# Four-layer image network on Trainium2: expectation values' products in one block, gathers two taps ahead, results consumed some steps later

## The chip, the cores and the metric

The kernel runs on one NeuronCore of one Trainium2 chip. The core has TensorE (PE: matrix products into PSUM), VectorE (DVE), ScalarE (ACT: activation functions), GpSimd (POOL: here it issues the gathers by index) and SyncE (SP: it issues all other transfers). Each works through its own list of instructions and waits at semaphores for the others. The metric is the time of one execution on the device, in microseconds (us); lower is better. Every number is float32.

## The reference, cut to what matters

The input is x of 16 images, 192 channels, 32 x 32 pixels. Four layers follow each other, each of the form x = x + layer(groupnorm(x)):

- layer 0: a recurrent block over the 1024 pixels, a linear layer, a 3 x 3 convolution, a batch norm over all images
- layer 1: attention. Each of 6 heads maps 32 channels of a pixel to 6 angles and these to a state of 64 amplitudes (a product of cosines and sines). Two fixed circuits w, one for queries and one for keys, turn the state; the squares of the amplitudes are probabilities, and their signed sums, projected to 4 numbers, are the query and key vectors. Softmax over the 1024 pixels follows
- layer 2: deformable convolution. A 3 x 3 convolution gives 18 offsets per pixel, and each of 9 taps reads the image at a shifted, fractional place (four corners with weights)
- layer 3: a gated feed-forward block with a 2 x 2 transform, a 3 x 3 convolution per channel and a GELU

The part of layer 1 that the first edit touches, in the reference:

```python
def _measure_z(state):
    probs = jnp.abs(state) ** 2
    return probs @ _ZSIGN.T
...
zq = _measure_z(_pqc(_pqc(state0, enc_w), q_w))
q_vec = _layernorm(zq @ q_proj_w.T + q_proj_b, ln_gamma, ln_beta)
```

The kernel folds the signs and the projection into one matrix `amat` of 64 amplitudes (real and imaginary part, so 128 rows) by 4 numbers.

## The kernel before, in words

**Two phases.** `phase_a` does layer 0 for all images and ends at about 3330 us. `phase_b`, which the change is in, does layers 1 to 3.

**Four streams.** `phase_b` ends with `weave`. It takes four generators, which issue instructions and yield a number at each pause: `vectors` (query and key vectors of layer 1), `attention` (its softmax), `layer2` (offsets, then gathers) and `layer3`. `weave` always continues the stream that has progressed least, where a yield counts as its number divided by the stream's weight. The weights are the sums of the yields of one image, so that all streams advance by one image at the same rate, and the third entries (1.27, 2.49, 3.78) hold each stream that many images behind the first. What `weave` gives is an order of priority. A scheduler in the layer below then puts each engine's instructions into a list, by that priority and by when it takes their operands to be ready, and it hands out buffers.

**Vectors.** For each image, three head pairs `pr` run one after the other. `products` builds the state `psi` of two heads on VectorE; TensorE transposes it (`ppsi`), ScalarE copies it (`psiT`). For the two circuits w and two halves of the pixels hf, TensorE applies the circuit (`pcirc`, L1059), and ScalarE squares it (`prob`, L1061, 128 x 1024: 512 pixels for each of two heads). The function `expect` (L1049) then makes `pz`: for each (w, hf) two matmuls of 128 rows by 32 columns by 512 pixels, one per head, added up in the 32 partitions of PSUM that start at q. The columns of `amat` that are used are shifted by head, so that head numbers land in different places and the sum keeps them apart. `expect` of one (w, hf) is issued one step after its Square; the four strips of 32 partitions are written at four different times. `pz` is allocated before the first circuit of the pair.

**Buffers.** In SBUF the tag `v4` has five buffers of 128 x 1024. It serves xb, y, vec1, vec2, psi and prob of `vectors` and xn and x1 of `attention`. In PSUM the tag `mm` has two banks of 128 x 512 for all small products (ppsi, pz, pxt, poffc, poff, pgn, pgv, pout, pdt and others), and `big` two tiles of 128 x 1024 for pmax, pscore, pcirc, paug and phad.

**Layer 2.** `layer2_offsets` normalizes, transposes and writes four shifted copies of the image as a table of rows to DRAM (`xg`), convolves for the offsets (`poffc`, L1303, four strips of 32 partitions for each of 9 taps), copies (`ot`, L1307), transposes (`poff`, L1310) and computes indices and weights on VectorE (`pos`, L1315, to `w4`, L1336). `layer2_gathers` goes through 4 blocks of pixels x 9 taps. For each tap GpSimd gathers two tiles `gt` (L1357, 6 buffers), ScalarE scales the first corner into `acc` (L1361, 5 buffers), VectorE adds three corners (L1387) and multiplies by the tap's weight (L1389), TensorE adds it up in PSUM (`pdef`, L1393).

**Group norm.** `groupstats` (L31 to L48) takes means on VectorE, averages over groups on TensorE (`pgn`), copies the result (`gm`, L37), and does the same for variances (`pgv`). All streams but attention use it.

**Layer 3.** `rows_in` makes four products `phad` (L1438); ScalarE scales two of them into `low` (L1445), VectorE combines with the others into `pad` (L1450); then come the convolution steps `dc` (L1487, L1489).

## Time and profile before

| | us |
|---|---|
| median of three runs | 9209.33 |
| lowest, highest | 9204.89, 9238.67 |
| the profiled execution, its own time | 9200.76 |
| its span, first to last instruction | 9199.0 |
| TensorE busy | 8010.2 (87%) |
| VectorE busy | 6945.0 (75%) |
| ScalarE busy | 4235.8 (46%) |
| GpSimd busy | 1784.4 (19%) |

The mean clock that TensorE was granted is 0.912 of full speed. By phase: from 0 to 3330 us TensorE is busy 3019.3 us and VectorE 2408.4; from 3330 to 8364 us (the last pz) 4464.3 and 3844.2 of 5034; from there to the end 526.5 and 692.4 of 835.

How to read the lines that follow: a group of instructions is given as line, engine, operation, output<-inputs with sizes, count, then busy time, mean duration in ns of one, and the idle time of the engine just before them with what ended most of it. A float32 matmul is recorded as two passes, so counts of matmuls in the profile are twice those of the program. Matmuls overlap: busy time is that of their union, and a mean duration is not a rate; the rate is read from one start to the next. In the stages' table the columns are the stretch, its length, and for each engine busy time and (count), then the granted clock, the DMA engines' mean busy share, and GB/s. A wait is given as engine, waiting tile and line <- releasing engine, tile and line: total us, times, longest us.

### The profile page before, as it was taken

Reading aid. Unit: us, or ns where it says so; the run is one execution under the profiler, and the core shown is the slowest. Engines: PE = TensorE matmul, PEld = TensorE weight load, DVE = VectorE, ACT = ScalarE, POOL = GpSimd, SP = SyncE. Lnnn points to the kernel's source line nnn. Section 1 sums busy time; section 2 is a strip of 40 time slices with the busy share of each in tenths; the row PEclk is TensorE's granted clock in tenths of the full one; section 3 lists DMA queues with packets and bytes.
Section 4 is the critical chain, followed back from the end, with each engine's and each line's share of the span. In section 5 each row is a group of like instructions: output and inputs, shape, how many; then the busy total and the mean of one; then the engine's idle time right before and its main releaser. Section 6 shows DMA issues by size and latency. Waiting matters only on the chain. (4 is left out here: it accounts for less than half of the span.)

```text
span 9199.0 us, 91391 instructions
## 1 busy us (share of the span) xinstructions
PE 8010.2 (87%) x30512; PEld 3387.7 (37%) x30512; DVE 6945.0 (75%) x14313; ACT 4235.8 (46%) x7395; POOL 1784.4 (19%) x1680
## 2 busy tenths in 40 slices
PE   5999999999999969998998988988988898988853
PEld 2555555555555532232333323323333233323221
DVE  6777777777777744668788778788788788778888
ACT  3444444444444424444454454444545444444432
POOL 0101000101001100222222222222222223223342
PEclk9899999999999979998998998999998998999965
DMA  1111111111111120433443443433333334334352
GB/s 50 43 43 45 44 43 50 43 43 46 44 43 50 40 55 21 136 122 103 125 129 95 134 124 100 128 115 117 119 118 119 118 113 124 120 103 131 118 159 64
DMA packets 301028, 814.44 MB, mean 89 GB/s; under 512 B 47579, under 2 KB 164381, under 8 KB 300555
## 3 DMA queue, kind: packets, MB, share of 16 engines
q0 software_dynamic: 92160, 453.06, 15.8%
q1 hardware_dynamic: 208395, 355.55, 12.4%
q8 instruction: 239, 3.92, 0.2%
q14 instruction: 234, 1.92, 0.1%
HBM read 667.13 MB, written 132.94 MB: 87 GB/s over the span
## 5 line engine op out<-in xcount | busy, mean ns | idle before, releaser
L1357 POOL DMA_INDIRECT gt<-xg,ix x1152 | 1463.8, 1271 | 4235.7 <-DMA xn<-xnd 1165.5
L1387 DVE SCALAR_TENSOR_TENSOR acc<-gt,w,acc 128x192 f32<-128x192 f32 x3456 | 1213.0, 410 | 173.4 <-ACT acc L1361 147.5
L1151 DVE TENSOR_REDUCE mx<-pmax 128x2 f32<-128x1024 f32 x768 | 934.8, 1218 | 431.8 <-PE pmax L1149 429.5
L1149 PE MATMUL pmax<-kt,qt 64*128 64x512 f32 x3072 | 1097.0, 671 | 174.2 <-ACT pexp L1191 83.6
L1188 PE MATMUL pscore<-qt,kt 64*128 64x512 f32 x3072 | 1017.7, 690 | 196.7 <-DVE mx L1151 109.7
L1191 ACT ACTIVATE pexp<-pscore 128x1024 f32<-128x1024 f32 x768 | 780.5, 1017 | 739.2 <-PE pscore L1188 732.3
L1361 ACT ACTIVATE acc<-gt,w 128x192 f32<-128x192 f32 x1152 | 497.9, 451 | 1281.2 <-DMA gt<-xg,ix 1007.5
L1180 PE MATMUL pav<-pexp,vo 128*64 128x512 f32 x3072 | 962.4, 658 | 80.9 <-ACT pexp L1191 57.2
L508 POOL COPY qbd<-qT 32x384 f32<-32x384 f32 x512 | 303.9, 594 | 2847.6 <-PE se L542 2762.7
L1489 DVE SCALAR_TENSOR_TENSOR dc<-pad,wdw,dc 128x512 f32<-128x512 f32 x1152 | 807.1, 742 | 9.5 <-ACT dc L1487 9.1
L1393 PE MATMUL pdef<-acc,ident 128*128 128x384 f32 x1152 | 597.3, 604 | 125.4 <-DVE acc L1389 111.1
L538 ACT ACTIVATE dm<-dm,wtm 128x128 f32<-128x128 f32 x1536 | 490.6, 388 | 348.0 <-DVE dm L494 268.6
L1149 PEld LDWEIGHTS pmax<-kt,qt 64*128 64x128 f32 x3072 | 315.6, 197 | 757.8 <-issue 202.1
L1188 PEld LDWEIGHTS pscore<-qt,kt 64*128 64x128 f32 x3072 | 286.5, 201 | 712.2 <-issue 300.8
L550 PEld LDWEIGHTS pintra<-v,pt 128*128 128x128 f32 x3072 | 428.6, 213 | 164.1 <-issue 71.0
L550 PE MATMUL pintra<-v,pt 128*128 128x33 f32 x3072 | 437.7, 291 | 2.4 <-DVE pt L545 2.4
L1180 PEld LDWEIGHTS pav<-pexp,vo 128*64 128x64 f32 x3072 | 172.0, 141 | 662.9 <-issue 504.1
L1393 PEld LDWEIGHTS pdef<-acc,ident 128*128 128x128 f32 x1152 | 194.2, 210 | 563.2 <-DVE acc L1389 225.1
L545 DVE SCALAR_TENSOR_TENSOR pt<-se,dm 128x512 f32<-128x512 f32 x384 | 263.0, 685 | 144.5 <-PE se L542 143.5
L1049 PE MATMUL pz<-prob,amat 128*32 128x512 f32 x768 | 366.5, 603 | 0.9 <-ACT prob L1061 0.9
L1061 ACT ACTIVATE prob<-pcirc 128x1024 f32<-128x1024 f32 x192 | 195.6, 1020 | 351.3 <-PE pcirc L1059 344.8
L542 PE MATMUL se<-qbd,kT 64*128 64x256 f32 x1536 | 292.4, 450 | 54.1 <-DVE pt L545 54.1
(423 smaller groups left out, 12848.3 us busy)
## 6 DMA issues: line engine op xcount, KB each, us to landing
dm<-gd SPq DMA_DIRECT2D x128, 768.0 KB
xg<-xt SPq DMA_DIRECT2D x224, 192.0 KB
gt<-xg,ix POOLq DMA_INDIRECT x1152
xb<-x_in SPq DMA_DIRECT2D x32, 384.0 KB
y<-ydram SPq DMA_DIRECT2D x32, 384.0 KB
x1d<-xb SPq DMA_DIRECT2D x32, 384.0 KB
xnd<-y SPq DMA_DIRECT2D x32, 384.0 KB
xn<-xnd SPq DMA_DIRECT2D x48, 256.0 KB
```

Of the source, the lines that this page charges most:

```text
L538: nc.scalar.activation(dm[:, h, :], dm[:, h, :], AF.Exp, bias=wtm[:, c, 64 + h:65 + h])
L550: nc.tensor.matmul(pa[:, hh * 33:hh * 33 + 33], pt[:, h * 128:(h + 1) * 128], v33[:, hh, :], start=True, stop=True)
L1149: nc.tensor.matmul(pm[:, hh, :], qT[r, tt * 128:(tt + 1) * 128], kT[r, hf * HS:(hf + 1) * HS], start=True, stop=True)
L1151: nc.vector.tensor_reduce(mx[:, tt, hf, :], pm, AX.X, ALU.max, negate=True)
L1180: nc.tensor.matmul(po[0][hh * 64:hh * 64 + 64], vo[:, tt, hh * 32:hh * 32 + 64], pe[:, hh * HS:(hh + 1) * HS], start=(tt == 0), stop=(tt = ...
L1188: nc.tensor.matmul(ps[:, hh * HS:(hh + 1) * HS], kT[r, tt * 128:(tt + 1) * 128], qT[r, s], start=True, stop=True)
L1191: nc.scalar.activation(pe, ps, AF.Exp)
L1357: nc.gpsimd.indirect_dma_start(out=gt, out_offset=None, in_=xg, in_offset=bass.IndirectOffsetOnAxis(ap=ix[:, c:c + 1], axis=0))
L1361: nc.scalar.activation(acc[:, j, :], gt[:, 0:192], AF.Copy, scale=w4[:, 0, c:c + 1])
L1387: nc.vector.scalar_tensor_tensor(acc[:, j, :], gt[:, cr * 192:(cr + 1) * 192], w4[:, cr, c:c + 1], acc[:, j, :], ALU.mult, ALU.add)
L1393: nc.tensor.matmul(po[:, 0:384], cn.ident, acc.rearrange("p j c -> p (j c)"), start=(t == 0), stop=(t == 8))
L1489: nc.vector.scalar_tensor_tensor(out, src, w, add, ALU.mult, ALU.add)
```

## The change

It has four parts.

1. In `vectors`, the four `prob` of a head pair are kept, and all eight matmuls into `pz` are issued together after the last Square: first the four strips for one head, then the four for the other. `pz` is allocated just before. `products` of the next pair is issued after this block instead of before the last `expect`. The pauses change from 2.5 to 2.0 after each circuit, and to 3.0 and 1.0 behind the block.
2. In `layer2_gathers`, `first` is split into `read` (the gathers) and `first` (ScalarE's scaling). The gathers of tap n + 2 are issued in the step of tap n, the scaling of tap n + 1 as before in the step of tap n. A pause of 4.0 stands between the first two reads and the first scaling.
3. Pauses are added before a result of another engine is used: 1.0 before the group means are copied; 3.0 before, 2.0 after and 4.0 later around the offsets' copy and transposes; 2.0 instead of 1.0 between `low` and `pad`.
4. The weights of three streams are set to the new sums of their pauses.

```diff
@@ groupstats
     nc.tensor.matmul(pg[:96, 0:2], cn.g6, mv[:, :, 0], start=True, stop=True)
+    yield 1.0
     gm = pool.tile([96, 2], F32, tag="gngm", name="gngm")
@@ phase_b
-        weave([(stream(0, vectors), 86.0), (attention(g), 205.8, 1.27), (layer2(g), 155.5, 2.49),
-               (stream(3, layer3), 131.9, 3.78)])
+        weave([(stream(0, vectors), 87.0), (attention(g), 205.8, 1.27), (layer2(g), 169.5, 2.49),
+               (stream(3, layer3), 136.9, 3.78)])
@@ vectors
-        pz = mm("pz")
-        def expect(w, hf, prob):
-            q = (w * 2 + hf) * 32
-            for hh in range(2):
-                o = 20 - (pr * 2 + hh) * 4
-                nc.tensor.matmul(pz[q:q + 32, :], g.amat[:, w, o:o + 32], prob[:, hh * HS:(hh + 1) * HS],
-                                 start=(hh == 0), stop=(hh == 1))
-        ready = None
+        prob = {}
         for w in range(2):
             for hf in range(2):
...
-                prob = v4("prob")
-                nc.scalar.activation(prob, pc, AF.Square)
-                yield 2.5
-                if ready:
-                    expect(*ready)
-                ready = w, hf, prob
+                prob[w, hf] = v4("prob")
+                nc.scalar.activation(prob[w, hf], pc, AF.Square)
+                yield 2.0
+        pz = mm("pz")
+        for hh in range(2):
+            o = 20 - (pr * 2 + hh) * 4
+            for w in range(2):
+                for hf in range(2):
+                    q = (w * 2 + hf) * 32
+                    nc.tensor.matmul(pz[q:q + 32, :], g.amat[:, w, o:o + 32], prob[w, hf][:, hh * HS:(hh + 1) * HS],
+                                     start=(hh == 0), stop=(hh == 1))
+        yield 3.0
         if pr < 2:
             psi = products(pr + 1)
-        yield 2.0
-        expect(*ready)
         if pr == 0:
...
+        yield 1.0
@@ layer2_offsets
         yield 2.0
+    yield 3.0
     ot = g.xp("ot")
     nc.scalar.activation(ot, po, AF.Identity)
+    yield 2.0
     pf = mm("poff")
...
+    yield 4.0
     n = 144
@@ layer2_gathers
-    def first(n):
+    def read(n):
         block, t = taps[n]
         part = []
-        acc = g.pairs("acc")
         for j in range(2):
...
+        return part
+    def first(part):
+        acc = g.pairs("acc")
         for j, gt, c in part:
             nc.scalar.activation(acc[:, j, :], gt[:, 0:192], AF.Copy, scale=w4[:, 0, c:c + 1])
-        return acc, part
+        return acc
...
-    coming = first(0)
+    reads = [read(0), read(1)]
+    yield 4.0
+    firsts = [first(reads[0])]
     for n, (block, t) in enumerate(taps):
-        (acc, part), coming = coming, first(n + 1) if n + 1 < len(taps) else None
+        if n + 2 < len(taps):
+            reads.append(read(n + 2))
+        if n + 1 < len(taps):
+            firsts.append(first(reads[n + 1]))
+        acc, part = firsts[n], reads[n]
@@ layer3, rows_in
                 nc.scalar.activation(low[j], ph[:, 1, j, :], AF.Copy, scale=g.fft[:, 2 + j, ab, gt:gt + 1])
-            yield 1.0
+            yield 2.0
```

## The prediction

> **What bounds the kernel now.** I read the page first (busy shares, slices, costliest groups), then the busy time by stretch of one steady image, the timeline of TensorE, and the waits by engine. The chain that ended last reaches back only to 9024 us, so it tells about the drain and not about the stretch that the change touches; I leave it aside. Lines of the page, busy tenths in 40 slices of 230 us, then the group that is re-ordered:

> ```profile
> PE   5999999999999969998998988988988898988853
> DVE  6777777777777744668788778788788788778888
> PEclk9899999999999979998998998999998998999965
> ...
> L1049 PE MATMUL pz<-prob,amat 128*32 128x512 f32 x768 | 366.5, 603 | 0.9 <-ACT prob L1061 0.9
> ```

> From slice 16 on (phase B, 3330 us to the end) neither engine is at 9 throughout: TensorE holds 8 to 9, VectorE 7 to 8. Over 3330 to 9199 they are busy 4991 and 4537 of 5869 us. So the question is which of the two is full where pz stands. The mapping of pz to images repeats: an image takes about 350 us (first gathers at 6522, 6870, 7225 us). The stretches of one image, from the view by stages:

> ```profile
> core 0: us, PE busy (x) PEld busy (x) DVE busy (x) ACT busy (x) POOL busy (x), PEclk, DMA share, GB/s
> 6570.00:6606.00 36.00, 34.99 (x123) 13.45 (x124) 24.46 (x48) 18.15 (x34) 6.04 (x7) 1.00 0.40 124
> 6606.00:6642.00 36.00, 30.49 (x105) 8.81 (x103) 34.65 (x70) 15.73 (x28) 9.76 (x6) 0.95 0.26 79
> 6690.00:6810.00 120.00, 99.42 (x321) 34.14 (x319) 114.27 (x228) 62.38 (x96) 30.13 (x24) 0.91 0.32 98
> 6785.00:6870.00 85.00, 81.57 (x325) 23.62 (x325) 58.49 (x102) 41.29 (x50) 3.66 (x4) 0.95 0.25 74
> 6870.00:6894.00 24.00, 21.79 (x68) 7.67 (x68) 20.48 (x52) 12.55 (x22) 16.61 (x13) 1.00 0.80 259
> ...
> ```

> The stretch without gathers (6785 to 6870, offsets being computed) is full on TensorE: 81.6 of 85 us, VectorE 58.5. In 6570 to 6606 TensorE is full too (35.0 of 36, VectorE 24.5). VectorE is the full one in 6690 to 6810 (114.3 of 120). The same view of pz alone gives 11.42 us x24 in 6785 to 6870, 6.06 us x13 in 6570 to 6606 with 1.55 just after, and 3.06 us x7 in 6870 to 6894: the 48 recorded pz matmuls of an image (12 products, two matmuls each, recorded as two passes) lie nearly all where TensorE is full.

> The timeline of TensorE shows what they cost next to a block of the same shape that is already on four strips, the offset convolution:

> ```profile
> 3730.80 1.90 PE L1049 MATMUL pz<-prob,amat 128*32 128x512 f32 x4
> 3732.64 1.13 PE L1149 MATMUL pmax<-kt,qt 64*128 64x512 f32 x4
> ...
> 3735.29 1.07 PE L1303 MATMUL poffc<-xpad,woff 96*32 96x512 f32 x8
> 3736.29 1.13 PE L1149 MATMUL pmax<-kt,qt 64*128 64x512 f32 x4
> ```

> From start to next start: 4 pz in 1.84 us, 0.46 each; 8 poffc in 1.00 us, 0.125 each. Both last 592 ns apiece; poffc overlaps about four at a time.

> [...] poffc here shows 3.7x for four. [...] 192 pz visits become 48, which no row prices, so I count nothing.

> **The change, part by part.** *Products in one block.* Before, a head pair has four visits of 1.84 us = 7.36. After, one visit of 8 matmuls, first the four strips of the first head, then of the second: the built order has 48 blocks of 8, none split. 16 passes at 0.125 = 2.0, with the tail of the last 2.1. Saved: 5.3 us a block, 3 x 16 blocks = 254 us of TensorE. That is the ceiling for this part. What is on the path:
> - 6785 to 6870, half the products: 11.0 us becomes 3.1, saved 7.9. TensorE is full, and the gathers wait for the offsets at its end. Two of the six products stand before 6810, where VectorE is full as well: I take off half of their 2.6, and count 6.6.
> - 6570 to 6606, four products: saved 5.3; VectorE has 11.5 us to spare: whole.
> - 6870 to 6894, two products: saved 2.6; VectorE is at 20.5 of 24: half, 1.3.

> Sum 13.2 us an image. In the VectorE-full stretches that follow nothing shrinks, and half-rate clock may take some back: I keep nine tenths, 11.9, times 16 images = 190 us. With all 5.3 of each block it would be 254, with the chain to the offsets alone (see the rivals) 96. The first images' products (from 3381 us) lie where TensorE is at 462 of 500 us, so they count alike. After the last pz (8364 us) the remaining 835 us stay.

> *Waits that the block adds.* It needs all four Squares. In the built order other matmuls stand between the last circuit product and the block; at the trace's rates 4.0, 8.7 and 6.8 us for the three head pairs. A Square lasts 1.02 us, so it is covered unless ScalarE is late. The next psi is issued behind the block; 11.4 and 16.4 us of matmuls stand before its transposes. Without that cover the price is what ScalarE is late by; behind pz on TensorE are the scores, and ScalarE's exponentials wait for those.

> *Buffers.* Four prob and vec2 fill all five v4 buffers, so the attention's xn load, x1 loads and psi are taken before or after a block. SyncE's order stays nearly the same; the second x1 load now has some 5 us of VectorE work ahead of its use instead of 13, and I count 0 to 1 us. In PSUM, pz holds one of the two mm banks for a block instead of a whole pair; waits such as pout for xo (16.6 us in 4500 us) shrink: at most 1 us an image.

> *Gathers two taps ahead, pauses and weights.* The waits in 4000 to 8500 us (13 images), from the waits by engine:

> ```profile
> ACT acc L1361 <- DMA gt<-xg,ix: 795.1, 431, 6.4
> ...
> DVE pos L1315 <- PE poff L1310: 197.7, 13, 15.3
> DVE pad L1450 <- ACT low L1445: 120.2, 40, 5.9
> ...
> DVE gngm L37 <- PE pgn L35: 61.0, 15, 6.1
> ...
> PE pscore L1188 <- DVE pad L1450: 24.1, 8, 5.9
> ```

> ScalarE waits 61 us an image for gathers, VectorE 15 for the offsets, 9 for low, 5 for the norm. By the text all of these should shrink. The built order says little moves: GpSimd still holds 72 gathers an image in the same order and six buffers; between a gather and its first reader stand 46 instructions of all engines on average instead of 43; VectorE reaches pos behind the same work plus one addition, pad behind low at 9 instead of 10, gngm at 7 instead of 6.5. ScalarE's wait is the one that TensorE feels (pexp behind acc). A tenth of 61 us less, a third of it felt: 2 us an image, 32 us in all at the high end, 0 or a few us lost at the low end (the pauses only move work). I take 10 us. The weights of the four streams only match the longer sums of their pauses.

> Sum: 9200.8 (the profiled execution; span 9199.0 and 1.8 around it) - 190 - 10 = 9001. The median of the runs (9209.3) stands 8.5 us above the profiled time, so about 9010; I say 9005, since both halves taken off above err to the slow side.

> **Rivals.** *More than the block:* moving work out of ScalarE's waits frees VectorE's stretches too, because one late gather stops all three (the waits for low and pad above are such cases). TensorE's six largest waits for ScalarE are 217 us in these 13 images, 16.7 each. If half of that goes as well: 8.3 x 16 = 133 less, about 8870. Against it: the built order hardly moves the gathers. *Given back in VectorE:* only the chain to the offsets gains. Five products stand before poff in its stretch, 9.2 us; after, one block and one more circuit product, 3.2: 6.0 us an image, 96 in all: 9113. For it: VectorE is busy 224 of the 263 us with gathers, and 114 of 120 after the first block. Against: the products are not there. *Slower:* the block becomes a wait. Its fourth Square stands in ScalarE's queue behind an acc, and TensorE stands still. It decides when the wait exceeds the 5.3 us saved; at the longest wait of acc for pdef, 6.9 us in every block, it costs 48 x 1.6 = 77: 9286. Against: the first pair's block, with the least cover, is in the stretch without gathers. *It doesn't do what it says:* the strips don't overlap with 128 rows as with 96: 9209. Against: pav, with 128 rows on two strips, already has 4 in 1.01 us, though each lasts about 0.6.

> **How the numbers follow.** Block as worked out 0.62 (own range 8940 to 9070), more 0.13, given back 0.13, slower 0.06, no overlap 0.06. About 0.5% (46 us) is what a measurement here can tell. The range takes in the likeliest case, the given-back case and half of the better one: 8880 to 9130. Faster by over 0.5%: the first three, less a little of the third, 0.87; within 0.5%: no overlap and that little, 0.07; slower 0.06.

> **What would show it.** Right: pz busy falls from 366 us to about 105, as 48 blocks of 16 in about 2 us; the stretch without gathers shrinks from 85 to about 77 us and an image from 350 to about 338; waits for pos and for gathers stay within a quarter. Wrong: blocks of 7 us (no overlap); TensorE idle before pz with prob as the releaser (slower); unchanged length with TensorE idle in its place and VectorE full (given back); waits of ScalarE for gathers halved (more).

## The result: half a per cent slower, with TensorE relieved as planned

| | before | after |
|---|---|---|
| median of seven runs, us | 9209.33 | 9261.55 |
| lowest, highest | 9195.97, 9238.67 | 9243.35, 9278.42 |
| profiled execution, its time and span | 9200.76, 9199.0 | 9250.15, 9248.3 |
| TensorE busy | 8010.2 | 7865.4 |
| mean granted clock | 0.912 | 0.904 |

The ratio is 1.0049, 95% interval 1.003 to 1.0068. I had forecast 9005, so the forecast was wrong by 257 us and in its sign.

The page of the changed kernel, busy tenths by slice as before:

```profile
PE   5999999999999969888888888888888888888853
DVE  7777777777777744767877778778678778778778
PEclk9899999999999979999898898998898998999865
```

From slice 17 on TensorE has fallen from "8 or 9" to 8 in nearly every slice. It has less to do, and the run is longer all the same. The group of the moved matmuls, from the groups by line of TensorE, and then TensorE's timeline at one block:

```profile
L1061 PE MATMUL pz<-prob,amat 128*32 128x512 f32 x768 | 96.0, 599 | 0.0
```

```profile
6829.88 1.92 PE L1061 MATMUL pz<-prob,amat 128*32 128x512 f32 x16
6831.73 1.13 PE L1146 MATMUL pmax<-kt,qt 64*128 64x512 f32 x4
```

So the block does what it says: 16 passes in 1.85 us to the next start, pz busy 96.0 in place of 366.5, and no idle time ahead of it (the last number of the group, 0.0). The stages of one image, gathers, then no gathers (the latter from the start of VectorE's last corner sum of an image to that of its first of the next); ahead of them the stretch with gathers of the kernel before:

```profile
core 0: us, PE busy (x) PEld busy (x) DVE busy (x) ACT busy (x) POOL busy (x), PEclk, DMA share, GB/s
6522.00:6785.00 263.00, 230.14 (x774) 82.57 (x772) 224.33 (x466) 130.89 (x218) 84.45 (x69) 0.92 0.44 134
...
6538.00:6807.00 269.00, 226.51 (x740) 82.14 (x739) 223.31 (x464) 132.75 (x219) 95.68 (x69) 0.88 0.42 130
6807.00:6896.00 89.00, 81.87 (x359) 24.39 (x356) 58.06 (x102) 42.77 (x52) 3.97 (x4) 0.95 0.24 71
```

The stretch without gathers took 85 us before and takes 89 here. The one with gathers has its TensorE 42 us short of full and a clock of 0.88, against 33 us and 0.92 before. One image is not the mean: over the ten images from the third to the twelfth the stretch without gathers grew from 85.1 to 91.5 us, and the one with gathers from 266.3 to 267.8. Waits in 4000 to 8500 us, first of ScalarE and VectorE, then of TensorE, and then two rows of TensorE's in the kernel before:

```profile
ACT acc L1363 <- DMA gt<-xg,ix: 834.3, 367, 8.7
...
DVE xo L1526 <- PE pout L1533: 230.9, 12, 19.2
...
DVE pad L1459 <- ACT low L1454: 104.2, 34, 5.1
...
DVE gngm L38 <- PE pgn L35: 89.6, 12, 8.9
PE pav L1177 <- ACT pexp L1188: 85.5, 32, 5.4
...
PE pcirc L1050 <- DVE mx L1148: 63.7, 27, 4.8
```

```profile
PE pav L1180 <- ACT pexp L1191: 26.7, 14, 3.9
...
PE pcirc L1059 <- DVE mx L1151: 0.9, 4, 0.2
```

VectorE's wait for pos (197.7 us in 13 times before) is down to 15.0 us in a single one, but in its place VectorE stands 19 us an image at xo, the instruction that is now ahead of pos, for pout. On TensorE, pav waited 26.7 us for the exponentials before and waits 85.5 now, and pcirc for the maxima 63.7 in place of 0.9. Not every wait grew: that of pscore for the maxima fell from 98.2 to 59.7.

To say where the time of an image went, I take from each trace the ten images from the third to the twelfth and split their mean length in three: *work*, TensorE's busy time with the part at half clock counted half; *half clock*, the other half of that part (the granted clock in these two traces is 1.0 or 0.5 at any time, in 316 spells before and 410 after); and *idle*, the rest. The three add up to the image by construction.

| us per image | image | work | half clock | idle |
|---|---|---|---|---|
| before | 351.4 | 288.2 | 25.3 | 37.9 |
| after | 359.2 | 276.2 | 31.5 | 51.5 |

Work fell by 12.0 us an image. Idle time grew by 13.6 and the loss to half clock by 6.2. Work is the time that TensorE was busy, which depends on how matmuls overlap, and is no constant of the program: over all the runs without the block it lies between 286.6 and 296.2 us, with the block and no other change of matmuls between 273.5 and 280.7.

### The profile page after: what moved, and what is told of

It reads as the page before. It is cut to its first block, busy times and chain, and to the rows that moved or that the text cites. A ratio compares the mean times of both kernels' runs of the same rounds, so it can differ in the third digit from the quotient of the medians.

```text
span 9248.3 us, 91393 instructions
## 1 busy us (share of the span) xinstructions
PE 7865.4 (85%) x30512; PEld 3365.6 (36%) x30512; DVE 6926.5 (75%) x14313; ACT 4283.4 (46%) x7433; POOL 1982.9 (21%) x1680
## 5 line engine op out<-in xcount | busy, mean ns | idle before, releaser
L1355 POOL DMA_INDIRECT gt<-xg,ix x1152 | 1660.9, 1442 | 4098.2 <-DVE w L1336 1790.3
L1146 PE MATMUL pmax<-kt,qt 64*128 64x512 f32 x3072 | 1075.4, 682 | 229.0 <-ACT pexp L1188 125.4
L1185 PE MATMUL pscore<-qt,kt 64*128 64x512 f32 x3072 | 1056.2, 687 | 161.1 <-DVE mx L1148 73.9
L1188 ACT ACTIVATE pexp<-pscore 128x1024 f32<-128x1024 f32 x768 | 780.3, 1018 | 803.8 <-PE pscore L1185 801.0
L1177 PE MATMUL pav<-pexp,vo 128*64 128x512 f32 x3072 | 1003.9, 671 | 121.4 <-ACT pexp L1188 116.3
L1498 DVE SCALAR_TENSOR_TENSOR dc<-pad,wdw,dc 128x512 f32<-128x512 f32 x1152 | 804.3, 742 | 15.3 <-ACT dc L1496 14.8
L1146 PEld LDWEIGHTS pmax<-kt,qt 64*128 64x128 f32 x3072 | 296.9, 198 | 831.0 <-issue 245.3
L1398 DVE TENSOR_TENSOR acc<-acc,wdef 128x384 f32<-128x384 f32 x576 | 317.1, 550 | 3.8
```

Source lines behind the costliest of these rows:

```text
L1146: nc.tensor.matmul(pm[:, hh, :], qT[r, tt * 128:(tt + 1) * 128], kT[r, hf * HS:(hf + 1) * HS], start=True, stop=True)
L1177: nc.tensor.matmul(po[0][hh * 64:hh * 64 + 64], vo[:, tt, hh * 32:hh * 32 + 64], pe[:, hh * HS:(hh + 1) * HS], start=(tt == 0), stop=(tt = ...
L1185: nc.tensor.matmul(ps[:, hh * HS:(hh + 1) * HS], kT[r, tt * 128:(tt + 1) * 128], qT[r, s], start=True, stop=True)
L1188: nc.scalar.activation(pe, ps, AF.Exp)
L1355: nc.gpsimd.indirect_dma_start(out=gt, out_offset=None, in_=xg, in_offset=bass.IndirectOffsetOnAxis(ap=ix[:, c:c + 1], axis=0))
L1498: nc.vector.scalar_tensor_tensor(out, src, w, add, ALU.mult, ALU.add)
```

## First round: which part lost it

Three theories. A: the pauses at the offsets push the transposes poff down TensorE's list, and the gathers wait for what follows from them. B: the block's gain is given back where VectorE is full. C: gathers two taps ahead collide with other transfers. For A stands TensorE's timeline after the last offset convolution:

```profile
6874.12 1.07 PE L1300 MATMUL poffc<-xpad,woff 96*32 96x512 f32 x8
...
6883.19 3.67 PE L1533 MATMUL pout<-gelu,wout 128*96 128x512 f32 x8
6886.70 0.60 PE L1309 MATMUL poff<-ident,ot 128*128 128x128 f32 x4
```

From the last poffc to poff it is 12.6 us. In the kernel before it is 3:

```profile
6858.04 1.07 PE L1303 MATMUL poffc<-xpad,woff 96*32 96x512 f32 x8
6859.03 1.08 PE L1180 MATMUL pav<-pexp,vo 128*64 128x512 f32 x4
6860.04 1.13 PE L1188 MATMUL pscore<-qt,kt 64*128 64x512 f32 x4
6861.10 0.66 PE L1310 MATMUL poff<-ident,ot 128*128 128x128 f32 x4
```

**The changed kernel without the offset pauses** (weight of layer2 160.5; in all runs the weights follow the sums of the pauses):

```diff
-    yield 3.0
     ot = g.xp("ot")
     nc.scalar.activation(ot, po, AF.Identity)
-    yield 2.0
     pf = mm("poff")
...
-    yield 4.0
     n = 144
```

> The changed kernel without the three pauses around the offsets' copy and transposes (3.0, 2.0, 4.0; layer2's weight 169.5 less 9 = 160.5), all else kept. Theory A, the pauses push the transposes poff some 10 us of matmul work behind the convolution (11.6 instead of 2.0 in the built order), and the gathers start that much later: the stretch without gathers falls from 90 to about 79 us, the time by 16 x 8 = 130 us to about 9130. Rival B, the loss is in the stretch with gathers, which VectorE fills: the time stays within 20 us of 9260. Rival C, the gathers ahead of time cost it: also about 9260.

Measured: 9048.38, ratio to before 0.9823 (0.9806 to 0.984). It is 213 us faster than the changed kernel and beats both kernels. That is more than A had forecast, though in the mean of the ten images the stretch without gathers fell by 8 us (91.5 to 83.5) and not by 11; the one with gathers fell by 9 (267.8 to 259.0). Its stages:

```profile
6778.00:7033.00 255.00, 221.44 (x764) 79.46 (x756) 225.25 (x469) 131.22 (x218) 85.14 (x69) 0.93 0.47 141
7033.00:7117.00 84.00, 79.84 (x337) 24.08 (x341) 56.52 (x99) 41.23 (x50) 3.30 (x4) 0.91 0.23 68
```

**The block alone** on the kernel before (edit: the block of the diff, nothing else; weight of vectors 86.0).

> The kernel before with the block of eight products alone (with its own pauses; the weight of vectors stays 86.0). Theory A with the gain as I predicted it: 9209 - 190 = about 9020. Rival B, the products' gain in the stretch with gathers is given back to VectorE and only the chain to the offsets gains, 5 to 6 us an image: about 9120. If the block is what makes the changed kernel slow: over 9240.

Measured: 9207.36, ratio 0.999 (0.9981 to 0.9999). Both A and B had expected a gain here, and the third line a loss. Neither came: the block alone earns nothing that counts.

**The offset pauses alone** on the kernel before (weight 164.5).

> The kernel before with the three offset pauses alone (layer2's weight 164.5). Theory A: poff stands 13.8 us of matmul work behind the convolution instead of 2.0, so 16 x 9 to 12 us more: 9350 to 9400. Rivals B and C: within 30 us of 9209.

Measured: 9406.11, ratio 1.0213 (1.0195 to 1.0231). The pauses cost 190 us without any other edit.

**One tap ahead** in the changed kernel:

```diff
-    reads = [read(0), read(1)]
-    yield 4.0
-    firsts = [first(reads[0])]
+    coming = first(0)
```

> The changed kernel with gathers issued one tap ahead as before, without the pause of 4.0 (layer2's weight 165.5). Theory A: within 30 us of 9260, since the offset pauses stay. Rival C, the gathers two taps ahead collide with other transfers (their mean issue time rose from 1271 to 1442 ns): about 9150.

Measured: 9127.1, ratio 0.9915 (0.9893 to 0.9937), 134 us faster than the changed kernel. It looked like C; it is not, as the last round shows. Nor does the time follow the gathers' own length, which C had pointed to: in the traces one takes 1442 ns in the mean in the changed kernel, but 1385 in a version below that takes 9092 us and 1343 in the one that takes 9406.

## Second round: the block's company

The block alone gives 0 and the version without offset pauses gives 168, so something beside the block matters. Four combinations without offset pauses:

> The kernel before with the block of products, the pause of 1.0 in the group norm and the pause of 2.0 in place of 1.0 after the low transform; one tap ahead, no pauses at the offsets (the planner's costs follow: 87.0, 156.5, 136.9). Without the offset pauses the change took 9048, and the block alone 9207, so some 159 us come from early gathers, from these two pauses, or from the block together with one of them. Gathers earn it: 9205, as the block alone. The two pauses earn it: about 9050. The block earns it, but only where something else fills TensorE's new gap 36 us into the stretch without gathers (2.1 us of idle there, then 17 to 20 us at half clock, in the block alone): about 9050 if these pauses fill it.

Measured: 9168.69, ratio 0.9945 (0.9926 to 0.9963).

> The kernel before with the block and the gathers two taps ahead (with their pause of 4.0; layer2 cost 159.5), without the other pauses. Gathers earn the 159 us: about 9050. The two small pauses earn it: 9205. The block with whatever fills the gap: about 9050 if two taps fill it; the gap stands outside the stretch with gathers, so I take 9170, by 10 us of half clock less in a fifth of the images.

Measured: 9134.61, ratio 0.9902 (0.9876 to 0.9928).

> The kernel before with the gathers two taps ahead alone (layer2 cost 159.5). Gathers earn it by themselves: about 9050, with the stretch with gathers 10 us an image shorter. The two pauses, or the block with something: 9210, within 30. Gathers two ahead collide (the 134 us that they cost beside the offset pauses): 9340.

Measured: 9272.89, ratio 1.0066 (1.0041 to 1.0091).

> The kernel before with the two small pauses alone (costs 87.0, 156.5, 136.9). The two pauses earn the 159 us by themselves: about 9050. Gathers earn it, or the block together with something: 9210, within 30.

Measured: 9353.03, ratio 1.0142 (1.0106 to 1.0178).

None of the single causes fits. Without the block each of these edits *loses* (55 and 135 us against 9218.2); with the block each pair *gains* (50 and 84). The gathers' part of the edit moves nothing by itself: in the traces GpSimd's instructions have the same order in the kernel before and in the two-tap version, one gather after another; how far they run ahead is held by the six buffers (from 4000 to 8500 us of the kernel before, GpSimd waited 935.2 us in 241 times for acc on VectorE, the last reader of a gt). What the run of the two-tap version measures is its pause of 4.0 and the weight that goes with it. (A pair of runs in the last round, one with one tap and one with two, bears this out.)

## Third round: what the block is worth in the changed kernel

The changed kernel without the block, and the best version without it:

> The changed kernel without the block: the four visits to one strip each, as before, with all the pauses and the gathers two taps ahead. The block is worth what my prediction priced (190 us) and the rest of the change lost it: 9450. The block's gain was given back by the stretch itself, as in the block alone: 9270, within 30. By my rows of the rest so far (two taps +56 and the two small pauses +137 on the kernel before, offset pauses +190) a plain sum gives 9600; I take 9450.

Measured: 9486.23, ratio 1.0304 (1.0279 to 1.033).

> The kernel before with the two small pauses and the gathers two taps ahead, without the block and the offset pauses (costs 87.0, 160.5, 136.9). With the block this took 9048. Effects add up: 9218 + 56 + 137 = 9411, and the block would be worth 360 here, more than its 254 of matmul time. The block is worth at most its matmul time where the other edits fill the gaps: 9230 to 9300.

Measured: 9254.39, ratio 1.0054 (1.0032 to 1.0075): 51 us lost against the 9203 of its set, where the two parts had lost 55 and 135 alone. The pauses do not add up, with the block or without.

By these pairs the block is worth 9486 - 9262 = 225 us in the changed kernel and 9254 - 9048 = 206 us in the best version, near the 190 that I had worked out. What else the change holds costs 9486 - 9203 = 283 us. The two together, 283 lost and 225 won, leave 58 us, close to the 52 that the changed kernel lost.

The block at unchanged order, but strip by strip inside:

```diff
-        for hh in range(2):
-            for w in range(2):
-                for hf in range(2):
+        for w in range(2):
+            for hf in range(2):
+                for hh in range(2):
```

> The changed kernel with the order of every instruction kept but within the block: the eight products go strip by strip, so that two neighbours share a strip and overlap less. A block should take some 4.6 us in place of 1.9 (five of eight steps of 0.92 one after another), so 48 blocks take 130 us more of TensorE. TensorE's work is what sets the time: 9390. The time that the block frees is lost in waits and half clock anyway: within 40 of 9260.

Measured: 9251.32, ratio 1.0055 (1.0037 to 1.0073). It doesn't test what it was meant to, since the block took no longer. TensorE's timeline:

```profile
6860.16 1.94 PE L1061 MATMUL pz<-prob,amat 128*32 128x512 f32 x16
6862.03 1.12 PE L1185 MATMUL pscore<-qt,kt 64*128 64x512 f32 x2
```

It serves as a second measurement of the changed kernel's order.

Of the offset pauses, the one behind poff alone:

> The changed kernel without the pauses of 3.0 and 2.0 ahead of the offsets' copy and transpose, but with the pause of 4.0 behind them (layer2 cost 164.5). The transposes poff now stand behind 2.0 us of matmuls after the last poffc in place of 11.6, with no pout among them. Loss by poff's late place: close to the run without any offset pause, 9048 to 9090. Loss by the late consumer (pos): 9230 or more. Loss by the sum of the pauses, wherever they lie: in proportion, 4 of 9, 9140.

Measured: 9082.5, ratio 0.9849 (0.9814 to 0.9884). That spoke for A: poff early, most of the loss gone.

## Fourth round: gap, place and sum

Two questions were left: why the block alone gains nothing, and whether the place of poff or only the sum of the pauses costs the time.

**The gap.** In the block alone, 36 us into the stretch without gathers of each steady image, TensorE runs dry where before a visit of pz stood. TensorE's timeline and then the stages, block alone:

```profile
7156.61 0.38 PE L1280 MATMUL pxt<-ident,xpad 96*128 96x96 f32 x2
7159.11 1.23 PE L1145 MATMUL pmax<-kt,qt 64*128 64x512 f32 x2 [2.12 <-DVE mx L1147]
```

```profile
7157.00:7179.00 22.00, 19.89 (x56) 5.34 (x56) 6.70 (x13) 8.91 (x12) 0.00 (x0) 0.61 0.41 118
```

2.1 us of idle are followed by half clock: the mean clock over 22 us is 0.61. I put transposes into the gap that write the same values again:

```diff
             for k in range(2):
-                nc.tensor.transpose(pv[:, (j * 2 + k) * 96:(j * 2 + k) * 96 + 96], flat[:, k, o:o + 128],
-                                    cn.ident[:96, :96])
+                for again in range(6 if t2 == 4 else 1):
+                    nc.tensor.transpose(pv[:, (j * 2 + k) * 96:(j * 2 + k) * 96 + 96], flat[:, k, o:o + 128],
+                                        cn.ident[:96, :96])
```

> The block alone, with the last two of an image's transposes pxt done six times in place of once (the same values into the same place; ten matmuls of 0.19 us more an image, 1.9 us), where TensorE idled 2.1 us in the block alone before 13 to 17 us at half clock; the order of everything else is kept. The half clock there takes the block's gain: the stretch without gathers loses 6 to 8 us, times the dozen images that have all stages, 9207 less 70 to 100: 9120. The gap is no cause (the half clock comes anyway, or another wait takes its place): 9207 to 9240.

Measured: 9087.81, ratio 0.9855 (0.9829 to 0.9882). Work was added and 120 us went. The same place in its trace, timeline and stage:

```profile
7087.11 1.21 PE L1281 MATMUL pxt<-ident,xpad 96*128 96x96 f32 x12
7089.29 0.66 PE L1038 MATMUL ppsi<-ident,psi 128*128 128x128 f32 x4 [0.97 <-ACT xt L1284]
```

```profile
7087.00:7109.00 22.00, 20.64 (x114) 6.51 (x112) 16.48 (x26) 13.33 (x17) 0.00 (x0) 1.00 0.43 126
```

The fill takes 0.83 us more (12 transposes in 1.21 us, 2 in 0.38), less than I had said. It also moved something, against what I had expected: one matmul of pmax that stood between pxt and the four ppsi now stands behind them, so TensorE doesn't wait for the maximum there. Both close the gap, from 2.1 us to 1.0, and this run doesn't part them. The 1.0 us that is left ends with xt, the copy of what pxt itself has written, which a longer pxt cannot shorten; so the swap may have done most of it. With the gap so short the clock stays whole there (1.00 over these 22 us), and the stretch falls from 91.7 to 81.5 us in the mean of ten images, with 8.6 us at half clock in place of 24.9. Of these 10.2 us, 8.2 are the half-clock loss (11.7 to 3.5 us by the split above). So half clock after a new gap had eaten a good part of the block's gain ("Why the prediction was wrong" has the rest). The same fill in the best version, where a gap of 1.7 us at that place is followed by 3.4 us of half clock:

> The same fastest version with the last two transposes pxt done six times. There the gap of 1.7 us is followed by only 3.4 us at half clock (1.7 us lost an image). Half clock follows the gap: 9048 less 14 times 1.7, 9025. The fill only adds its 1.9 us of work: 9048 to 9075.

Measured: 9076.25, ratio 0.984 (0.9812 to 0.9867): 28 us slower than without by the medians, though the intervals of the two ratios overlap; an image is 1.1 us longer, 0.8 of it the fill's own time. This run could not show what closing that gap is worth. Its gap lies ahead of pmax, and so ahead of the transposes, and the fill leaves it as it was:

```profile
7078.19 1.76 PE L1146 MATMUL pmax<-kt,qt 64*128 64x512 f32 x4 [1.72 <-DVE mx L1148]
7079.88 2.18 PE L1282 MATMUL pxt<-ident,xpad 96*128 96x96 f32 x12
```

It is 1.7 us long with the fill and without, and the loss to half clock in the stretch without gathers stays too (5.5 us and 5.4). What the run prices is a fill in a place where it closes nothing.

**Place or sum.** Late poff without the pause behind it:

> The changed kernel without the pause of 4.0 behind the transposes poff, but with those of 3.0 and 2.0 ahead of them (layer2 cost 165.5). On TensorE's list 13.8 us of matmuls, four pout among them, stand between the last poffc and poff, against 11.6 in the changed kernel and 2.0 to 3.0 without these two pauses. Loss by poff's late place: 9230 to 9290, with poff some 12 to 15 us after the last poffc. Loss by the late consumer, or by the sum of pauses: 9120 to 9180.

Measured: 9127.09, ratio 0.9893 (0.986 to 0.9925), on the side of the sum: poff stands 14 us after the last poffc, as late as ever, and 134 us are gone. In the traces this version has the same order of instructions on ScalarE, GpSimd and SyncE as the one-tap version above, which took 9127.1, and on TensorE and VectorE but for a few near-simultaneous neighbours: the pause of 4.0 taken out at either place is the same edit, and one tap or two makes no difference. Then the offsets hurried in the best version (the pause after the last poffc left out too):

> The fastest version so far (9048: block, two taps, the two small pauses, no offset pauses) with the pause of 2.0 after the last poffc left out too (layer2 cost 158.5), so that poff stands behind 0.5 us of matmuls in place of 3.0. The stage is a chain that ends in the offsets, each us of it a us an image: poff 2 us earlier, 12 to 14 images, 9020. TensorE then waits for ScalarE's copy at poff for about 1 us and gains nothing: 9048, within 20.

Measured: 9188.51, ratio 0.9967 (0.9952 to 0.9981). Both expectations missed: poff comes 2 us sooner after poffc, and 140 us are lost. It is no chain in which a us counts as a us. The last two runs set place against sum:

```diff
-    yield 3.0
     ot = g.xp("ot")
...
-    yield 2.0
     pf = mm("poff")
...
     left.ix, left.w4 = ix, w4
-    yield 6.0
+    yield 11.0
```

> The changed kernel with its pauses of 3.0 and 2.0 moved from ahead of the offsets' copy and transpose to behind the indices (6.0 becomes 11.0), so that the sum of layer2's pauses stays 169.5 and poff comes at once. poff's late place costs the time, 170 us of it: 9082, within 30. The sum of the pauses, which sets how the other streams are laid beside layer2, costs it: 9250, within 30.

Measured: 9246.75, ratio 1.0033 (1.0017 to 1.0048).

> The changed kernel with the pauses of 3.0 and 2.0 alone: the two of 4.0 are gone (layer2 cost 161.5), and poff still stands behind 12.8 us of matmuls, four pout among them. poff's late place costs the time by itself: 9200 or more. The sum of the pauses costs it (160.5 gave 9048, 164.5 gave 9082, 165.5 gave 9127, 169.5 gave 9251): about 9060.

Measured: 9092.02, ratio 0.9857 (0.9839 to 0.9875).

Poff at once with the whole sum is as slow as the changed kernel; poff late with a small sum is 44 us behind the best and 170 ahead of the changed kernel. Theory A falls. All versions that hold the block and the two small pauses, by the sum of layer2's pauses, with the time from the start of the last poffc to poff (the times are of several sets of runs, in which the kernel before had medians of 9203 to 9218):

| version | sum | poffc to poff, us | time | image | work | half clock | idle |
|---|---|---|---|---|---|---|---|
| one tap, no offset pauses | 156.5 | 3.5 | 9168.7 | 352.4 | 280.6 | 24.4 | 47.4 |
| offsets at once | 158.5 | 1.5 | 9188.5 | 353.3 | 275.9 | 25.7 | 51.6 |
| no offset pauses | 160.5 | 3.5 | 9048.4 | 342.6 | 279.5 | 22.2 | 40.8 |
| late poff, less | 161.5 | 13.0 | 9092.0 | 345.4 | 280.7 | 20.8 | 44.0 |
| late pos only | 164.5 | 2.6 | 9082.5 | 344.3 | 278.3 | 23.6 | 42.4 |
| late poff only | 165.5 | 14.1 | 9127.1 | 347.2 | 278.1 | 27.0 | 42.2 |
| pauses behind | 169.5 | 2.6 | 9246.8 | 357.5 | 275.7 | 30.3 | 51.4 |
| changed kernel | 169.5 | 12.1 | 9261.6 | 359.2 | 276.2 | 31.5 | 51.5 |

The two versions with the sum 169.5 agree in idle time, in half clock and in TensorE's two largest waits, with poff at 12.1 and at 2.6 us. Where poff is late, the stretch without gathers is longer (91.5 us against 79.7) and the one with gathers shorter (267.8 against 277.8). The same trade stands between "late poff, less" and "no offset pauses": about 12 us longer without gathers (96.0 against 83.5), about 10 shorter with them (249.4 against 259.0). So theory A saw a true effect, but most of it comes back in the other stretch. TensorE's waits from 4300 to 8000 us in the run with the pauses behind:

```profile
PE pmax L1146 <- ACT pexp L1188: 92.8, 51, 2.6
PE pav L1177 <- ACT pexp L1188: 63.4, 23, 5.5
```

For the changed kernel the same rows have 90.2 and 67.2 us. What the sum does follows from `weave`: the larger it is, the smaller a share of an image each gather step counts, so less work of the other streams is laid beside each of them. That this is why TensorE then waits more was not tried by itself. In all runs the weight followed the sum, so the pauses and the weight are not parted either. And below 160.5 the time rises again; the table shows a best place, not a law.

## Why the prediction was wrong

**Step "products in one block": right in size, wrong as a gain that stands alone.** 16 passes take 1.85 us where I said 2.0 to 2.1; pz lost 270 us where I said 254. On the time it was worth 225 and 206 us in company against 190 worked out. But I counted stretches where TensorE is full as if freed time there were gained whole, and kept a tenth for half clock and the like. In the block alone an image's work fell by 14.7 us (288.2 to 273.5), and half clock took 9.2 of it (25.3 to 34.5) and idle time 9.1 (37.9 to 47.0). "TensorE busy 81.6 of 85" hid that its matmuls wait for maxima and exponentials in turn. A visit of pz had stood in such a wait, and when it left, the wait came out, with the clock's fall behind it. The run with that gap closed won back the half clock (25.4), and not the idle time (46.8).

**Step "waits that the block adds": right.** pz has 0.0 idle ahead of it. **"Buffers": right as far as seen.** TensorE's wait of pout for xo, 16.6 us before, has no row among the largest; the loads were not priced apart.

**Step "gathers two taps ahead, pauses and weights": the step that failed.** It said "0 or a few us lost at the low end (the pauses only move work)" and took 10 us of gain. In place of that gain stands a loss of 283 us. The gather edit does move nothing; I had seen that GpSimd's order is the same, and should have taken 0. The pauses and their weights cost the 283 us together without the block, and the offset pauses alone 190. I had looked at how many instructions stand between a producer and its reader, on VectorE's list for pos. I hadn't looked at TensorE's list, where 11.6 us of matmuls in place of 2.0 now stood ahead of poff. Had I done so, I would have told a true thing and given it the wrong price, as theory A did. The price, as far as these runs show, lies in that a pause of layer2 and the weight that follows it re-lay *all* streams against each other: "The weights of the four streams only match the longer sums of their pauses" was the sentence that hid it.

**The rivals.** Slower: 9286 was near the time, but its mechanism, TensorE idle before pz, isn't there. Given back: its sign is seen in part (idle TensorE in the stretch with gathers), but VectorE is no fuller there (223.3 of 269 us, 224.3 of 263 before), and the stretch without gathers didn't shrink either, so it was no more right. No overlap and more were plainly wrong: 16 passes in 1.85 us, and a wait for gathers that grew. Of what I said would show it, pz busy and the wait for gathers (5% more) came as told; the wait for pos (nearly gone, with xo's in its place), the stretch (85 to 77) and the image (350 to 338) did not.

**What stays open:** which single wait makes the order at 169.5 worse than at 160.5, and whether it is the pauses or layer2's weight. The two small pauses, in the group norm and after low, were only tried together. The waits of the changed kernel and of the version at 160.5 differ in many rows at once: pav for exponentials 67 against 49 us in 3700, pqub for y 25 against no row, pcirc for maxima 54 against 81 the other way.

## What to carry to other kernels

Where a planner lays streams beside each other by pauses and weights, a pause is never local: price it by building and running it, one edit at a time and in pairs, because here edits that lose alone (55 and 135 us) gain beside another (84 and 50). Before counting freed matmul time as gained, ask what TensorE will find in that place; if it is a wait, saved time can turn into idle time, and half clock behind it can take a large part of what was saved (in the block alone 14.7 us of work an image went, 9.1 us of idle time and 9.2 of half clock came). A fill closes a gap only if it stands in it: look at which side of the wait it lands. And look whether an edit that "issues earlier" changes an engine's own list: one tap or two left the lists all but the same here, and the time too (9127.1 and 9127.09).

## What the runs showed of the hardware

| busy share of the slice | slices | next slice at half clock |
|---|---|---|
| under 40% | 91 | 91 |
| 40 to 50% | 61 | 47 |
| 50 to 60% | 62 | 13 |
| over 60% | 1570 | 19 |

The recorded busy share doesn't explain all of them: of the 19 slices in the last row, ten were busy throughout, and each of these held 14 to 18 of pqub, matmuls of only 18 columns (in the 921 fully busy slices after which the clock held, 0.1 in the mean). Nor does pqub decide it: in the changed kernel seven fully busy slices at full clock with 14 of them were followed by full clock and one by half.

Gaps shorter than a slice were enough here. The gap of 2.1 us in the block alone was followed by 13 to 20 us at half clock (17 of the 22 us whose mean clock is 0.61 above): up to 10 us lost for 2 us of gap. The gap of 2.8 us at that place in the changed kernel was followed by half clock in 9 of 11 images, where one slice took most of it and was 27 to 42% busy. In the other two it fell on two slices, both over half busy (63 and 54%, 66 and 52%), and the clock held.

**How long half clock lasted.** Of the 170 spells of half clock that begin between 4300 and 8000 us, 169 lasted one to five slices and one lasted six. Of 86 slices at half clock that were under 80% busy none was followed by full clock; of 261 that were 98% busy or more, 155 were.

**Strips.** Four strips of 128 rows by 32 columns ran side by side, four matmuls in the time of one (16 passes in 1.85 us in the changed kernel, 4 in 1.84 before), also where the program put neighbours on the same strip (16 passes in 1.87 us, strip by strip). The trace doesn't tell which strip a record belongs to, so whether they were put in another order on the way stays open.

**Repeatability.** Two programs with the same instruction order, measured at different times, had medians of 9127.1 and 9127.09. So close an agreement is luck: the single times lie between 9112 and 9140, and between 9098 and 9134.
